# One layer of convolution blocks and experts on one core: the first norm in halves, fifteen weight loads moved beside the first scans, and the order of the expert tiles' pieces, patterns and result transfers changed

## The chip, the cores and the metric

The kernel runs on 1 core of one Trainium2 chip. The metric is the device time in microseconds (us) of one execution; for the kernel before it is the median of 3 runs. Engines are named as the profile names them: PE (TensorE), DVE (VectorE), ACT (ScalarE), POOL (GpSimd), and SP (SyncE), which here only issues DMAs.

## The reference

Four images of 256 channels and 32x32 pixels (1024 positions) go through one convolution block and one mixture of experts. Everything is float32. Cut to what matters:

```python
# conv block, per image; xs: 1024 positions x 256 channels, already normalised over C
xn = layernorm(xs)                                  # again, with norm_w, norm_b
xc = 4 branches of 64 channels
# one branch (mamba), 128 inner channels, 16 states:
u, z = split(xc @ inw.T);  u = silu(causal_conv4(u))
dt, Bm, Cm = u @ xpw.T;    dt = softplus(dt @ dtw.T + dtb)
h[t] = exp(dt[t]*A) * h[t-1] + dt[t]*u[t]*Bm[t]     # the selective scan, t = 0..1023
y[t] = sum over states of h[t]*Cm[t]
xm = (y + u*D) * silu(z) @ outw.T + skip*xc
# then: sigmoid gate Q over the branches, three 1-d convolutions with products (r, f),
# local convolution || 8-head attention over 1024 positions, product fc, layernorm, gelu,
# norm over the image, 3x3 depthwise convolution, layernorm, product proj
x = x + conv_block(ln_c(x))
# experts: t = 4096 tokens x 256
t = t + MoE(ln_t(t))   # 8 experts, top 2 by softmax, 256 -> 1024 -> gelu -> 256
```

## The kernel before

**Stages.** `network()` places all weights, then everything is emitted under one `tc.manual_schedule`, so that on each engine the instructions run in the order in which the Python code calls them. The order is made by hand: the scans are the main line, and generators carry the other work beside them. `beat()` advances every running generator by ticks: each `yield n` asks to be left alone for n ticks, `pace(b, f)` changes how many ticks a generator of image b gets for one beat, and a generator's first beat advances it twice.

**Weights.** `load` puts each weight on a queue named in the call (SP, ACT or POOL) ahead of everything else; `wqkT_s`, `qk_b`, `vb`, `fcT_s` and others are among them. Six short preparations follow (`ob`, `prb`, `projT_s`, `fcm`, `fcT_s`, `fcb`: small products on PE, sums and scalings on DVE). `weights()` (L251) then builds `inwk`, the in-projection with the four taps of the causal convolution folded in (per branch a scaling `diag` on DVE, matmuls on PE, a copy on DVE), and `wd` from transposes of `xpw`.

**The opening.** `normalised(b)` (L382) fetches the image x in one DMA on SP, forms mean, centred values, squares, variance and root for each half of 512 positions (the squares on POOL), scales over the whole width with POOL and DVE, and stores `xl` in `XL`, a copy in DRAM for later. `first_part()` (L602) does for image 0, branch 0: both halves of `up` (`project_u`, 16 matmuls, L439), both silus, one load of the logarithm's function table on ACT (`log_exp`), `project_dt` (L470), `softplus`, `sum_dt` and `times_u` on POOL, and `spread_dt` (L499): DMAs on SP which broadcast dt over the states, through DRAM.

**The scans.** A part is one image, one branch, one half of 512 positions; 4x4x2 = 32 parts of 16 steps. A step holds the decay exp(dt*A) on ACT (L531), two groups of `dBu` (L538) and scan (L545) on DVE, the product with Cm (L550) on POOL with a copy of the last column (L549), and the sum over states as matmuls (L556). `scan(at, i, stop)` (L631) mixes in the next part's projections by three tables (`before`, `behind`, `group`).

**Beside the scans.** While image b is scanned, the generators of image b-1 (convolutions, attention, `joined`, `around`, `sent_off`) run. After the last scan, image 3's own chain stands alone: attention, product (`joined`), norm, 3x3 taps, norm, routing. Beside it run the pieces of expert tiles whose rows are there.

**Experts.** `dispatch` (L1435) computes the two experts of each token of an image, then sends its rows into `XS`, sorted by expert, by 16 indirect DMAs on POOL (L1560), each behind a small `memset` of a tile `apart`. `blank_ends` (L1389) writes 8 sets of blank rows behind the last counts, on ACT's queue, for the last image. The tiles of 256 rows come in `SERIES` (8, 8, 23): series s can start when the counts of image s+1 are known. `tiles()` (L1088) walks through them; its `load` calls `series`, which makes the table of tiles (`tiles_of`, `table`, L1582 to L1620; patterns by iota on POOL at L1582 and L1603, comparisons on DVE). Tile 15 is held until image 3's rows are sent (L1144). Each tile is emitted in 8 pieces, so many ticks apart as `PACE` (L1211) says for the stage in which image 3's chain is:

```python
PACE = {"product": 3, "norm": 1.7, "taps": 0.67, "rows": 1.6}
```

`tile()` (L1769) does 32 matmuls `h` (L1778), gelu on ACT (L1783), 32 matmuls `y` (L1788), the weighting `ys` (L1798) and two indirect DMAs on POOL which add 128 rows each to `Y` in DRAM (L1799); the second waits for the first, since both write `Y`. The last four tiles run only if the counts need them. `bring_back` (L1805) reads `Y` back (L1810) and adds it to the tokens.

Of the kernel before, what the change touches and what calls it, by code (L numbers as in the profile page):

```python
# [9 lines left out]
F32 = mybir.dt.float32  # L10
# [13 lines left out]
NHC = DFF // P  # L24

# [46 lines left out]
def network(  # L72
# [34 lines left out]
    def ps_tile(name):  # L107

        return psum.tile([P, HALF], F32, tag="ps", name=name)
# [33 lines left out]
    with tc.tile_pool(name="w_conv", bufs=1) as wp, tc.tile_pool(  # L143
# [11 lines left out]
        def load(ap, name, eng):  # L155
            t = wp.tile(list(ap.shape), F32, name=name)
            eng.dma_start(t, ap)
            return t
# [3 lines left out]
        moutT_s = load(moutT, "moutT_s", nc.scalar)  # L162
        qdwT_s = load(qdwT, "qdwT_s", nc.gpsimd)
        qpwT_s = load(qpwT, "qpwT_s", nc.gpsimd)
        rpwT_s = load(rpwT, "rpwT_s", nc.gpsimd)
        fpwT_s = load(fpwT, "fpwT_s", nc.gpsimd)

        wqkT_s = wp.tile([P, NC2, 4, P], F32, name="wqkT_s")
        for ci in range(NC2):
            nc.sync.dma_start(  # L170
                wqkT_s[:, ci].rearrange("p w (i x) -> p (w i) x", x=2 * HD)
                .rearrange("p c (i x) -> p c i x", x=HD),
                wqkT[:, ci].rearrange("p c (i x) -> p c i x", x=2 * HD)[:, :, :, 0:HD],
            )
        qk_b = wp.tile([P, 4], F32, name="qk_b")
        for i in range(4):
            at = _AT["qk_b"] + i // 2
            nc.scalar.dma_start(
                qk_b[ts(i, HD), :], vecs[ds(64 * (i % 2), HD), at : at + 8 : 2]
            )  # L180
        wvT_s = load(wvT, "wvT_s", nc.gpsimd)
        aoutT_s = load(aoutT, "aoutT_s", nc.gpsimd)
        fcT_s = load(fcT, "fcT_s", nc.sync)
        projT_s = load(projT, "projT_s", nc.gpsimd)

        vb = wp.tile([P, NC2], F32, name="vb")
        nc.scalar.dma_start(vb, vbias.rearrange("a (c p) -> p (a c)", p=P))
        ob = wp.tile([P, NC2], F32, name="ob")
        obp = ps_tile("obp")
        for co in range(NC2):  # L190
            for ci in range(NC2):
                nc.tensor.matmul(
                    obp[:, co : co + 1], aoutT_s[:, ci, ts(co, P)], vb[:, ci : ci + 1],
                    start=(ci == 0), stop=(ci == NC2 - 1),
                )
        nc.vector.tensor_tensor(
            ob, obp[:, 0:NC2], V[:, _AT["attn_outb"] : _AT["attn_outb"] + NC2], ALU.add
        )

        prb = wp.tile([P, NC2], F32, name="prb")  # L200
        prp = ps_tile("prp")
        for co in range(NC2):
            for ci in range(NC2):
                nc.tensor.matmul(
                    prp[:, co : co + 1], projT_s[:, ci, ts(co, P)], col("norm_b", ci),
                    start=(ci == 0), stop=(ci == NC2 - 1),
                )
        nc.vector.tensor_tensor(
            prb, prp[:, 0:NC2], V[:, _AT["proj_b"] : _AT["proj_b"] + NC2], ALU.add
        )  # L210
        for ci in range(NC2):
            nc.vector.tensor_scalar(
                projT_s[:, ci, :], projT_s[:, ci, :], col("norm_w", ci), None, ALU.mult
            )

        fcm = wp.tile([P, 2 * NC2, 1], F32, name="fcm")
        nc.vector.tensor_reduce(fcm, fcT_s, AX.X, ALU.add)
        nc.vector.tensor_scalar(fcm, fcm, 1.0 / C, None, ALU.mult)
        nc.vector.tensor_tensor(
            fcT_s, fcT_s, fcm.to_broadcast([P, 2 * NC2, C]), ALU.subtract  # L220
        )
        fcb = wp.tile([P, NC2], F32, name="fcb")
        fbp = ps_tile("fbp")
        for c in range(NC2):
            nc.tensor.matmul(
                fbp[:, 0:1], ones_mean, col("fc_b", c), start=(c == 0), stop=(c == NC2 - 1)
            )
        nc.vector.tensor_tensor(
            fcb, V[:, _AT["fc_b"] : _AT["fc_b"] + NC2], fbp[:, 0:1].to_broadcast([P, NC2]),
            ALU.subtract,  # L230
        )
# [141 lines left out]
        LEFT = KC - 1  # L373

# [5 lines left out]
        XN, XM = {}, {}  # L380

        def normalised(b):  # L382


            xn = XN[b] = act8.tile([P, NC2, N + LEFT], F32, tag="a8", name=f"xn_{b}")
            nc.gpsimd.memset(xn[:, :, 0:LEFT], 0.0)
# [4 lines left out]
            nc.sync.dma_start(xn[:, :, LEFT:], x[b].rearrange("(c p) n -> p c n", p=P))  # L391
# [92 lines left out]
        def sum_dt(b, n, h):  # L484
            both = T[b, n, h, "dt"] = actd.tile([P, 2, HALF], F32, tag="dt", name=f"dt_{b}_{n}_{h}")
            nc.gpsimd.tensor_tensor(both[:, 0, :], T[b, n, h, "low"], T[b, n, h, "over"], ALU.add)

        def times_u(b, n, h):
            both = T[b, n, h, "dt"]
            nc.gpsimd.tensor_tensor(  # L490
                both[:, 1, :], both[:, 0, :], T[b, n, "u"][:, half(h)], ALU.mult
            )
# [109 lines left out]
        def first_part():  # L602

            for h in range(2):
                project_u(0, 0, h)
            u = T[0, 0, "u"] = a4("u_0_0")
            for h in range(2):
                nc.scalar.activation(
                    u[:, half(h)], T[0, 0, h, "up"], AF.Silu, bias=col("convb", 0)
                )  # L610
            loaded[0] = None
            log_exp()
            project_dt(0, 0, 0)
            softplus(0, 0, 0)
            sum_dt(0, 0, 0)
            times_u(0, 0, 0)
            for g in range(GD):
                spread_dt(0, 0, 0, g)
            for h in range(2):
                project_c(0, 0, h)  # L620
                copy_c(0, 0, h)
            spread_c(0, 0, 0, 0)
            spread_b(0, 0, 0, 0)
            for h in range(2):
                project_z(0, 0, h)
                copy_z(0, 0, h)
            T["z"] = [(0, 0, "z")]
            for i in range(LEAD):
                decay(0, 0, 0, i)
# [416 lines left out]
        def sent_off(b):  # L1046
# [32 lines left out]
            pace(b, PACE["rows"])  # L1079
            yield from experts.dispatch(  # L1080
                b, xr, act8.tile(experts.XR, F32, tag="a8", name=f"XR_{b}"), root,
                log_exp,
            )
# [4 lines left out]
        def tiles():  # L1088
# [5 lines left out]

            def known(n):
                return experts.counted >= B - 3 + order[n][0]
# [4 lines left out]
            def load(n):  # L1101
                s, i = order[n]
                if i == 0:
                    tables.append(experts.series(
                        s, lambda name, shape: act2.tile(shape, F32, tag="a2", name=name)
                    ))
# [32 lines left out]
            for n in range(len(order)):  # L1139
# [3 lines left out]

                while n == sum(experts.SERIES[:2]) - 1 and not sent(n + 1):  # L1144
                    ahead(n + 1, 0)
                    yield 1
# [64 lines left out]
        PACE = {"product": 3, "norm": 1.7, "taps": 0.67, "rows": 1.6}  # L1211
        with tc.manual_schedule(engines=ALL):
            log_exp()
            start(normalised(0), weights())
            drain()
            first_part()
            for b in range(B):
                for p in range(PARTS):
                    at = b * PARTS + p
                    stop = b > 0 and p == PARTS // 2 - 1 or at == len(parts) - 1  # L1220
                    if b == 0 and p == 2:
                        start(normalised(1))
# [65 lines left out]
class Experts:  # L1288
# [9 lines left out]

    T = 256
# [6 lines left out]
    def __init__(self, ctx, tc, psum, B, b1, ident, eps5, ones_mean, Wg, bg, W1, W2, b2, out):  # L1306
# [13 lines left out]
        self.Y = md.tile([NTOK + P, C], F32, name="Y")  # L1320
        m0 = self.m0 = ctx.enter_context(tc.tile_pool(name="moe0", bufs=1))

        blank = self.blank = m0.tile([P, self.ROW], F32, name="blank")
        nc.gpsimd.memset(blank, 0.0)
        nc.gpsimd.iota(
            blank[:, C : C + 1], [[0, 1]], base=NTOK, channel_multiplier=1,
            allow_small_or_imprecise_dtypes=True,
        )
        nc.gpsimd.memset(blank[:, C + 3 : C + 4], -1.0)
        nc.scalar.dma_start(self.Y[ds(NTOK, P), :], blank[:, 0:C])  # L1330
# [43 lines left out]
        self.counted = -1  # L1374
        self.read = []
        self.blank_rows(self.SPARE)

    def blank_rows(self, at):

        ins = self.nc.scalar.dma_start(  # L1380
            self.XS[ds(at, self.T), :].rearrange("(n p) c -> p n c", p=P),
            self.blank.rearrange("p (a c) -> p a c", a=1)
            .to_broadcast([P, self.T // P, self.ROW]),
# [51 lines left out]
    def dispatch(self, b, X1, XR, root, log_exp):  # L1435
# [120 lines left out]
        apart = m0.tile([P, 1], F32, tag="apart", name=f"apart_{b}")  # L1556
# [21 lines left out]
    def tiles_of(self, temp, name, rows, base=0):  # L1578

        nc, K = self.nc, self.NTOK // self.T  # L1580
        steps = temp(f"steps_{name}", [P, NE, K])
        nc.gpsimd.iota(  # L1582
            steps, [[0, NE], [self.T, K]], base=base, channel_multiplier=0,
            allow_small_or_imprecise_dtypes=True,
        )
# [5 lines left out]
    def table(self, temp, keep, name, n, ntile, done=None):  # L1591
# [10 lines left out]
        which, past = temp(f"which_{name}", S), temp(f"past_{name}", S)  # L1602
        nc.gpsimd.iota(  # L1603
            which, [[1, n], [0, NE]], base=0, channel_multiplier=0,
            allow_small_or_imprecise_dtypes=True,
        )
# [28 lines left out]
    def series(self, s, temp):  # L1635
# [10 lines left out]
        ntile = self.tiles_of(temp, s, self.count[:, :, b : b + 1], 0 if last else T - 1)  # L1646
        if s:
            nc.vector.tensor_tensor(ntile, ntile, self.done, ALU.subtract)
        table, starts, ends = self.table(temp, self.kept, s, n, ntile, self.done if s else None)
# [119 lines left out]
    def tile(self, j, got, hs, ys):  # L1769
# [27 lines left out]
        for t in range(2):  # L1797
            nc.vector.tensor_scalar(ys[:, t, :], ys[:, t, :], wgt[:, t, :], None, ALU.mult)  # L1798
            nc.gpsimd.indirect_dma_start(  # L1799
# [3 lines left out]
            )  # L1803

# [122 lines left out]
```

## Time and profile before

| | us |
|---|---|
| runs | 2487.04, 2480.68, 2478.96; median 2480.68 |
| profiled execution, own time | 2486.92 (span 2485.2, mean granted PE clock 0.913) |
| first `dBu` (L538) / first scan (L545) | 80.13 / 80.93 |
| last group of `dBu` (L538) | 1676.3 |
| image 3 behind its attention: product, norm, taps, norm, routing | 1964 to 1992, 2020, 2044, 2083, 2110 |
| counts of image 3 known | 2109.94 |
| one expert tile in the last stretch | 14.25 |
| last result transfer issued / read-back issued | 2450.47 / 2455.74 |

All times come from the one profiled execution; its own time is 6.2 us above the median of the runs. Over the whole span PE is busy 85%, DVE 65%, ACT 48% and POOL 45%, but the shares differ by stage: DVE carries the scans, PE the attention and the tiles. In a row of the timeline the columns are start, duration, engine, line, operation, output<-inputs, shapes, count, and in brackets the idle time of the engine just before, with what ended it. PEclk is the share of full speed that the throttle granted to PE.

### The profile page before, as it was taken

How to read it: one execution, taken by the hardware profiler on the slowest of the kernel's cores; microseconds unless marked ns; L12 is line 12 of the kernel's file. 1: busy time of each engine (PE TensorE's matmuls, PEld its weight loads, DVE VectorE, ACT ScalarE, POOL GpSimd, SP SyncE). 2: the span in 40 equal slices, each digit the busy share in tenths (PEclk: the TensorE clock that was granted, in tenths of full speed). 3: DMA queues.
4: the chain of work that ended last, by engine and by line, in shares of the span. 5: the costliest groups of instructions: out<-in, count | busy, mean ns of one | idle time of the engine just before them, and what ended most of it. 6: DMA issues, size and time to landing. Idle time of an engine off the chain costs nothing. (4 is left out here: it accounts for less than half of the span.)

```text
span 2485.2 us, 28288 instructions
## 1 busy us (share of the span) xinstructions
PE 2122.3 (85%) x8810; PEld 941.7 (38%) x8810; DVE 1622.3 (65%) x2243; ACT 1193.9 (48%) x2016; POOL 1111.8 (45%) x1163
## 2 busy tenths in 40 slices
PE   5776778899977799998589999758999999599995
PEld 2121112333311132232013223204773477588884
DVE  2688998876799887789978877985424354111211
ACT  1544455368663647765253686413427654122221
POOL 2577777541577661176775405562112011322221
PEclk8799997899998889997788999868999999899997
DMA  3443342220243321033333202334431154566664
GB/s 95 99 109 93 96 117 70 72 70 27 51 103 97 75 61 34 28 105 98 97 80 77 57 18 51 90 100 145 115 112 36 55 154 142 176 195 196 190 195 148
DMA packets 154541, 244.17 MB, mean 98 GB/s; under 512 B 34017, under 2 KB 103301, under 8 KB 154377
## 3 DMA queue, kind: packets, MB, share of 16 engines
q1 hardware_dynamic: 133856, 215.46, 30.7%
q0 software_dynamic: 13744, 19.31, 3.8%
q10 hardware_dynamic: 6776, 7.45, 0.9%
q8 instruction: 74, 1.21, 0.2%
q14 instruction: 91, 0.74, 0.1%
HBM read 141.16 MB, written 33.85 MB: 70 GB/s over the span
## 5 line engine op out<-in xcount | busy, mean ns | idle before, releaser
L550 POOL TENSOR_TENSOR hs<-hs,cs 128x512 f32<-128x512 f32 x512 | 669.5, 1309 | 222.0 <-DVE hs L545 175.1
L556 PE MATMUL yp<-hs,quads 128*32 128x512 f32 x1024 | 344.5, 684 | 173.1 <-POOL hs L550 123.2
L531 ACT ACTIVATE dA<-dts,A 128x512 f32<-128x512 f32 x512 | 342.9, 713 | 291.6 <-DMA dts<-dt 185.7
L538 DVE TENSOR_TENSOR dBu<-dts,bs 128x512 f32<-128x512 f32 x512 | 348.1, 680 | 80.5 <-DMA dts<-dt 24.2
L545 DVE TENSOR_TENSOR_SCAN hs<-dA,last,dBu 128x512 f32<-128x512 f32 x256 | 327.7, 1280 | 24.9 <-DVE dBu L538 0.5
L1799 POOL DMA_INDIRECT Y<-ys,dest x70 | 112.6, 1609 | 512.7 <-DVE ys L1798 362.2
L545 DVE TENSOR_TENSOR_SCAN hs<-dA,dBu 128x512 f32<-128x512 f32 x256 | 312.5, 1221 | 30.6 <-ACT dA L531 5.7
L1783 ACT ACTIVATE hs<-h,b 128x256 f32<-128x256 f32 x280 | 117.0, 471 | 405.5 <-PE h L1778 265.6
L871 ACT ACTIVATE e<-st 128x512 f32<-128x512 f32 x512 | 263.1, 606 | 87.2 <-PE st L861 86.7
L1788 PE MATMUL y<-w,hs 128*128 128x256 f32 x1120 | 259.6, 383 | 4.8 <-ACT hs L1783 4.8
L1778 PE MATMUL h<-xT,w 128*128 128x256 f32 x1120 | 253.2, 382 | 0.8 <-DVE xT L1756 0.8
L1788 PEld LDWEIGHTS y<-w,hs 128*128 128x128 f32 x1120 | 212.2, 192 | 43.4 <-issue 10.1
L1778 PEld LDWEIGHTS h<-xT,w 128*128 128x128 f32 x1120 | 213.3, 191 | 40.2 <-issue 9.7
L1756 DVE COPY xT<-xp 128x512 f32<-128x512 f32 x35 | 24.2, 692 | 297.8 <-PE xp L1755 297.8
L556 PEld LDWEIGHTS yp<-hs,quads 128*32 128x32 f32 x1024 | 55.6, 117 | 429.0 <-POOL hs L550 287.4
L523 PE MATMUL bs<-u,xpwT_s 128*32 128x512 f32 x1024 | 176.9, 670 | 40.6 <-DVE hs L545 23.6
L549 POOL COPY last<-hs 128x1 f32<-128x1 f32 x256 | 66.3, 259 | 318.0 <-DVE hs L545 309.5
L913 DVE TENSOR_TENSOR e<-e,e 128x512 f32<-128x512 f32 x256 | 171.4, 732 | 53.9 <-PE av L903 44.0
L861 PE MATMUL st<-qk 32*128 32x512 f32 x1024 | 194.0, 655 | 6.8 <-DVE hs L545 4.5
L439 PE MATMUL up<-xn,inwk 64*128 64x512 f32 x256 | 131.7, 659 | 15.6 <-DVE hs L545 9.2
L903 PE MATMUL av<-e,v 128*32 128x512 f32 x1024 | 142.7, 621 | 0.0
L861 PEld LDWEIGHTS st<-qk 32*128 32x128 f32 x1024 | 68.1, 188 | 132.4 <-issue 88.1
(271 smaller groups left out, 2499.3 us busy)
## 6 DMA issues: line engine op xcount, KB each, us to landing
w<-in_W_dram SPq DMA_DIRECT2D x136, 512.0 KB, 4.0
dts<-dt SPq DMA_DIRECT2D x512, 128.0 KB, 2.4
cs<-cd SPq DMA_DIRECT2D x512, 64.0 KB, 2.0
xs<-XS SPq DMA_DIRECT2D x35, 260.0 KB, 4.5
b<-in_b_dram SPq DMA_DIRECT2D x35, 128.0 KB, 4.2
xn<-in_x_dram SPq DMA_DIRECT2D x4, 1024.0 KB, 5.7
XL<-xl SPq DMA_DIRECT2D x8, 512.0 KB, 2.8
xl<-XL SPq DMA_DIRECT2D x4, 1024.0 KB
```

What stands on the lines that cost most here:

```text
L523: nc.tensor.matmul(bs[r], xpwT_s[:, n, s : s + 1].to_broadcast([P, 32]), T[b, n, "u"][:, half(h)], start=True, stop=True,)
L531: nc.scalar.activation(dA, T[b, n, h, "dts", g][:, 0, :], AF.Exp, scale=A[:, g, n, q : q + 1])
L538: nc.vector.tensor_tensor(dBu, T[b, n, h, "dts", g][:, 1, :], T[b, n, h, "bs", q], ALU.mult)
L545: nc.vector.tensor_tensor_scan(hs, T[b, n, h, "dA", i], dBu, 0.0 if h == 0 else last, ALU.mult, ALU.add)
L550: nc.gpsimd.tensor_tensor(hs, hs, T[b, n, h, "cs", q], ALU.mult)
L556: nc.tensor.matmul(T[b, n, h, "yp"][ts(g, 32)], quads, T[b, n, h, "hs", q * GD + g], start=(q == 0), stop=(q == GS - 1),)
L861: nc.tensor.matmul(sts[i], k[r, ts(kt, P)], q[r, half(h)], start=True, stop=not shifted)
L871: nc.scalar.activation(es[i], sts[i], AF.Exp, scale=1.0 / HD**0.5)
L903: nc.tensor.matmul(accs[0][ts(i, HD)], v8[:, kt, ts(4 * g + i, HD)], es[i], start=(kt == 0), stop=(kt == NK - 1),)
L913: nc.vector.tensor_tensor(first[i], first[i], es[i], ALU.add)
L1778: nc.tensor.matmul(hp[:, i, :], w1(c, k), xT[:, c, :], start=(c == 0), stop=(c == NC2 - 1))
L1788: nc.tensor.matmul(yp[:, ts(t, C)], hs[:, k, ts(t, P)], w2(k), start=(k == 0), stop=(k == NHC - 1))
```

## The change

Five parts of the code change; the work itself stays the same.

1. **Opening.** x of image 0 is the first DMA on SP, in two pieces of 128 channels. A new `first_normalised()` works on image 0 in halves throughout: the squares are taken by ACT, all scaling by DVE. `start(weights(), first_normalised())` replaces `start(normalised(0), weights())`. `first_part` does half 0 from `up` to the spreads of dt before half 1's `up`, with `sum_dt` and `times_u` on DVE; silu and the logarithm's table are loaded twice.
2. **Weights.** Calls of `load` without a queue go on a list; a generator `later_weights()`, started with the first scan part, issues them on SP, one for each tick, and then does the six preparations.
3. **Patterns.** `count_up` makes the two iotas of a series in advance: for series 0 when `tiles()` starts, for series 1 and 2 at the third tile of the series before.
4. **Result transfers.** The two indirect DMAs of a tile no longer wait for one another (each follows those of the tile before), with a memset of `apart` between them. Blank rows get distinct targets, so `blank` and `Y` grow by 128 rows.
5. **Pieces.** Other numbers in `PACE`, a stage "routing" of its own, and "rows" from the counts on; tile 15 is not held back any more.

```diff
+        place_xn(0)          # xn_0: memset of 3 columns on POOL, two DMAs on SP
+        later = []
...
+        def load(ap, name, eng=None):
             t = wp.tile(list(ap.shape), F32, name=name)
-            eng.dma_start(t, ap)
+            if eng is None:
+                later.append((t, ap))
+            else:
+                eng.dma_start(t, ap)
...
+        def later_weights():
+            nc.sync.dma_start(vb, vbias.rearrange("a (c p) -> p (a c)", p=P))
+            for t, ap in later:
+                nc.sync.dma_start(t, ap)
+                yield 1
...          # wqkT_s in 2 DMAs, qk_b in 4, then ob, prb, projT_s, fcm, fcT_s, fcb
+        def first_normalised():
+            xn = XN[0]
...
+            mean = [column_mean(f"mean_0_{h}", [part(c, h) for c in range(NC2)]) for h in range(2)]
+            var = []
+            for h in range(2):
+                sq = [a2(f"sq_0_{h}_{c}") for c in range(NC2)]
+                for c in range(NC2):
+                    nc.vector.tensor_tensor(part(c, h), part(c, h), mean[h], ALU.subtract)
+                    nc.scalar.activation(sq[c], part(c, h), AF.Square)
+                var.append(column_mean(f"var_0_{h}", sq))
+                yield 1
...
+            for h in range(2):
+                root(r1[:, half(h)], var[h], eps6)
+                root(r2[:, half(h)], var[h], eps11, scale=1.0 + 1e-5)
+                for c in range(NC2):
+                    nc.vector.tensor_tensor(xl[c][:, half(h)], part(c, h), r1[:, half(h)], ALU.mult)
+                    nc.vector.tensor_tensor(part(c, h), part(c, h), r2[:, half(h)], ALU.mult)
+                    nc.vector.tensor_scalar(
+                        part(c, h), part(c, h), col("norm_w", c), col("norm_b", c),
+                        ALU.mult, ALU.add,
+                    )
+                yield 1
...
         def first_part():
+            u = T[0, 0, "u"] = a4("u_0_0")
             for h in range(2):
                 project_u(0, 0, h)
-            u = T[0, 0, "u"] = a4("u_0_0")
-            for h in range(2):
                 nc.scalar.activation(
                     u[:, half(h)], T[0, 0, h, "up"], AF.Silu, bias=col("convb", 0)
                 )
-            loaded[0] = None
-            log_exp()
-            project_dt(0, 0, 0)
-            softplus(0, 0, 0)
-            sum_dt(0, 0, 0)
-            times_u(0, 0, 0)
-            for g in range(GD):
-                spread_dt(0, 0, 0, g)
+                loaded[0] = None
+                log_exp()
+                if h == 0:
+                    project_dt(0, 0, 0)
+                    softplus(0, 0, 0)
+                    sum_dt(0, 0, 0, nc.vector)
+                    times_u(0, 0, 0, nc.vector)
+                    for g in range(GD):
+                        spread_dt(0, 0, 0, g)
...
-            pace(b, PACE["rows"])
-            yield from experts.dispatch(
+            pace(b, PACE["routing"])
+            for ticks in experts.dispatch(
...
+                if experts.counted == b:
+                    pace(b, PACE["rows"])
+                yield ticks
...
+            experts.count_up(0, temp)
+            yield 5
...
-                while n == sum(experts.SERIES[:2]) - 1 and not sent(n + 1):
-                    ahead(n + 1, 0)
-                    yield 1
+                if order[n] in ((0, 2), (1, 2)):
+                    experts.count_up(order[n][0] + 1, temp)
...
-        PACE = {"product": 3, "norm": 1.7, "taps": 0.67, "rows": 1.6}
+        PACE = {"product": 4, "norm": 2.2, "taps": 0.9, "routing": 2, "rows": 0.75}
...
-            start(normalised(0), weights())
+            start(weights(), first_normalised())
...
+                    if b == 0 and p == 0:
+                        start(later_weights())
...
-        blank = self.blank = m0.tile([P, self.ROW], F32, name="blank")
+        blank = self.blank = m0.tile([P, T // P, self.ROW], F32, name="blank")
...
+    def count_up(self, s, temp):
...
+        self.numbers[s] = steps, which
...
-            nc.gpsimd.indirect_dma_start(
+        added = []
+        for t in range(2):
+            if t:
+                nc.gpsimd.memset(self.apart, 0.0)
+            ins = nc.gpsimd.indirect_dma_start(
                 out=self.Y[:, :],
...
+            for other in added:
+                self.tc.declare_no_dep(ins.ins, other.ins, reason="no two share a row")
+            self.follow(ins, self.added, "a row may be added to by both")
+            added.append(ins)
+        self.added = added
```

## The prediction

> **What bounds the kernel now.** I read the page first, then the busy time by stage, then the timeline of the first 130 us, of the last scan part and of everything behind the scans, and the waits of PE. The page's chain that ended last covers only the final 2 us, so the bound has to be read stage by stage.
>
> ```profile
> PE 2122.3 (85%) x8810; PEld 941.7 (38%) x8810; DVE 1622.3 (65%) x2243; ACT 1193.9 (48%) x2016; POOL 1111.8 (45%) x1163
> ```
> ```profile
> core 0: us, PE busy (x) PEld busy (x) DVE busy (x) ACT busy (x) POOL busy (x), PEclk, DMA share, GB/s
> 50.00:75.00 25.00, 20.76 (x31) 6.80 (x32) 2.45 (x2) 8.25 (x12) 7.98 (x6) 0.52 0.11 43
> 300.00:400.00 100.00, 76.86 (x231) 17.92 (x232) 93.92 (x101) 50.43 (x75) 77.46 (x88) 0.91 0.40 100
> 2300.00:2400.00 100.00, 100.00 (x479) 88.06 (x478) 17.96 (x59) 23.51 (x56) 21.59 (x14) 1.00 0.67 194
> ```
> No engine bounds the opening (DVE 2.45 of 25 us), DVE bounds the scans (94%), PE bounds the expert tiles at the end (100%).
>
> ```profile
> 34.41 2.82 PE L343 MATMUL mean<-xn,ones_mean 128*128 128x512 f32 x4
> 54.24 14.02 PE L439 MATMUL up<-xn,inwk 64*128 64x512 f32 x16 [6.35 <-POOL xn L421]
> 68.19 2.07 PE L470 MATMUL dtp<-u,wdt 128*128 128x512 f32 x2
> 75.56 10.14 SPq L499 DMA_DIRECT2D dts<-dt  x16
> 80.13 0.70 DVE L538 TENSOR_TENSOR dBu<-dts,bs 128x512 f32<-128x512 f32 x1 [22.71 <-DMA dts<-dt]
> ```
> The opening is one chain of latencies: mean, norm, both halves of up, dt, spread, first scan at 80.93. Nothing overlaps it.
>
> ```profile
> 1642.81 0.29 DVE L1586 TENSOR_TENSOR steps<-count,steps 128x128 f32<-128x128 f32 x1 [5.37 <-POOL steps L1582]
> 1649.13 1.27 POOL L550 TENSOR_TENSOR hs<-hs,cs 128x512 f32<-128x512 f32 x1 [6.18 <-DVE hs L545]
> ```
> In the last part the first tile table needs a pattern that sits behind scans and row transfers on POOL: DVE waits 5.37 us for it, then POOL 6.18 us for DVE.
>
> ```profile
> 2126.26 3.03 ACT L1783 ACTIVATE hs<-h,b 128x256 f32<-128x256 f32 x8 [15.52 <-DMA XS<-blank]
> 2126.78 3.72 PE L1788 MATMUL y<-w,hs 128*128 128x256 f32 x16 [2.83 <-ACT hs L1783]
> 2167.15 1.12 PE L1755 MATMUL xp<-ident,xs 128*128 128x128 f32 x4 [22.40 <-DMA xs<-XS]
> 2445.90 1.54 POOL L1799 DMA_INDIRECT Y<-ys,dest  x1 [7.79 <-DVE ys L1798]
> 2450.47 1.54 POOL L1799 DMA_INDIRECT Y<-ys,dest  x1 [3.03 <-DMA Y<-ys,dest]
> 2455.74 6.59 SPq L1810 DMA_DIRECT2D yy<-Y  x7
> ```
> Behind the attention of the last image PE stands 2.83 us for ACT, which queues behind eight blank-row transfers, and 22.4 us for the first rows of series 2. The last two result transfers follow one another 4.57 us apart, and the read-back follows the second.
>
> **Opening.** x now goes out first and later weights do not share the way; PE's first taps need only V and `every`. gm ends at 7.75 (row); in `beat` both generators advance twice on their first tick, so PE then runs two taps (2.06 each, DVE inwk 0.68 and diag 0.67 between): 13.3, by when x (1 MB, 8.6 us from issue under the old load) is in. Mean 2.82 and 1.88; centring of half 0 1.29, squares on ACT 2x0.57, var 1.9, four root steps 2.6: 22.8. DVE's six scaling passes (0.62 each, from 1.23 for 1024) and diag end at 27.4, the fourth taps at 28.4, four rounds of xpw and wd (37.08 to 42.6 with other work, 1.03 each) at 32.6. Eight up matmuls for half 0 at the 0.876 of the row, 7.0: 39.6. Silu 0.7 and the table load 1.28 (before it was paid after both halves), dtp 2.07, softplus 2.53 (70.31 to 72.84), two sums on DVE at 0.68 in place of 1.27 and 1.26 on POOL: the first dt spread leaves at 46.7 instead of 75.56. ACT now decides: up of half 1 ends at 49.5, its silu at 50.2, and a second pair of table loads (2x1.28) is added. From the second silu to the last z copy took 68.99 to 77.28, 8.3 us; 0 to 2.5 of it, the softplus, falls out, and the first decay (0.72) follows. The first scan starts at 57 to 60; I take 58.7, 22.2 us earlier. By then the spreads have landed: scans 0 to 4 took 9.5 us (80.93 to 90.44), paced by dts, and will take 4x1.92 = 7.7: 1.8 more. Together 24.0.
>
> The unknown is PE's clock in `up`. The row has it at half speed for 14 us of unbroken work (PEclk 0.50 from 52 to 72); at 106 us eight took 3.70. If half 0 and half 1 ran like that, 3.3 each and 1 of dtp go, about 8 us more. I take the slow row: the same xpw rounds, with PE nearly idle, stand ahead of it.
>
> The Trainium skill, page "TensorE: Matmul & The Clock Gate", Part 1, says that about 3.4 us of sustained matmuls return the clock to full. The row of `up` does not agree (16 matmuls of 64 rows, 14 us, never faster). By the rule half 0 would take an estimated 5.3 us and half 1 3.5, and the forecast would be some 6 us lower.
>
> **Weights beside the scan.** DVE gets fcm 1.22+0.16, fcT 1.22, ob, prb and fcb 0.16 each, projT 0.35+0.34: 3.8 us, in part 1, where it is busy 31.6 of 33.4 us: all of it on the path. PE's 4.6 us (obp, prp, fbp) hide, PE being at 77%. SP gets fifteen issues: wqkT 2.82, qk_b 4.35 and vb 0.45 (their old rows), fcT 0.4 to 2.98, seven others at 0.43 (weight issues of the tiles): 11 to 13.6 us, ahead of cs of quads 2 and 3 and of the dts of part 1. SP issues about 25 of part 0's 36 us, so it just fits; the last dts group lands about when step 3 of part 1 needs it. Cost 0 to 4, I take 1; if the cover were gone, all 13.6. The 2.4 MB find DMA at 59% share. XL[0] and the second x issue cost nothing: no one waits. Net opening: 24.0-3.8-1 = 19.2 (12 to 29).
>
> **Patterns.** The iotas of table 0 come five ticks before the table. DVE's 5.37 and POOL's 6.18 are one stall; the table's 4.2 us on DVE stay, but POOL (2.52 us a step against DVE's 1.98) hides most. Gain 5 (2 to 6). The two held act2 buffers leave 15; attention needs about 13. Free.
>
> **Result transfers.** The second of a tile's two no longer waits for the first. In the middle PE covers both already (14.25 us a tile). At the end 4.57 becomes 1.54 plus a memset (0.4 with its gap): 2.3 gained (1 to 3).
>
> **Tile pieces.** I counted the yields. Product, norm, taps, norm, routing have 12, 17, 10, 21, 19 ticks. At paces 3/1.7/0.67/1.7/1.6 that places tile 13, piece 5 at the count; at 4/2.2/0.9/2.2/2 it is tile 12, piece 1: 12 pieces, 22 us of PE (1.81 each), move behind the count, and 0.75 then puts tile 15 at the last row transfer without its wait. PE work is the same; only its idle time counts. Before: 7.6 in the stages, 2.83, 22.4 = 33. After:
> - Stages: the chain gets 13 us shorter, not 22: the taps alone are 20 us of DVE (16x1.25) and 4 of the tiles', over 11 pieces (20 us of PE). Idle 13 (9 to 20).
> - Blank rows: ACT's block (11.3 from the counts' end) now falls on pieces 1 or 2, where PE has only one or two h pieces left and y needs ACT: 9 (3 to 12).
> - First rows of series 2: load is still called from tile 15, its DVE work behind that tile's predecessor: ys 1.5, table 4.9, SP 5.3 (2155.3 to 2160.6), landing 6.5, against 10.8 of PE: 7.4 (3 to 9).
>
> Sum 29.4: 3 gained (-9 to +17).
>
> **Sum.** 19.2+5+2.3+3 = 29.5. The profiled execution took 2486.92 (span 2485.2), 6.2 above the median of the three runs, so its successor would be 2457.4; against the median 2480.68, **2451**.
>
> **Rivals.** *Tail as meant*: blank block covered as now and stage idle still 7.6; 15 of 33 idle remains, 18 gained in place of 3: 2436. For it: ACT's 15.5 us cost PE only 2.83 before. Against: the counted piece. *Fast halves*: up at 3.3 us less each: 2443. *Queue full*: all of SP's 13.6 on the scan, the tail at -9: 24-17.4+5+2.3-9 = 5 gained, 2476. *Starved PE* (slower): behind the attention the moved pieces leave pure idle, 22; the blank block goes uncovered, 12.7 more; the 22.4 stays; clock drops add 5: 40 lost against 26.5 gained elsewhere, 2494. It decides from 26.5 us of added idle between 1964 and 2170; against it, the stages held waits on PE (var, ACT behind gelu) that shrink. *Not as said*: x still arriving late behind POOL's memset would leave the opening near 70 us, about 2470.
>
> **Numbers.** Mine 0.56, tail as meant 0.20, fast halves 0.10, queue full 0.06, starved 0.06, not as said 0.02. About 0.3% (7.4 us) can be told from no change. Faster 0.88, same 0.06, slower 0.06. Range 2427 (6, 2.6 and some 15 more from tail or clock) to 2471 (opening 12 and the tail at its low end); queue full and starved lie outside.
>
> **What would show it.** First scan near 59; up in two runs of 8 at 0.88 with dtp between; no 5.37 in the last part; DVE 4 us longer in part 1; xs wait below 10, a wait of y on ACT near 9; result pairs 2 us apart. Wrong if the first scan starts after 70, or the idle time of PE behind the attention leaves 24 to 42.

## The result, and the profile after

The changed kernel takes 2480.34 us (median of 4), the kernel before 2480.61: ratio 0.9995, interval 0.9977 to 1.0013. No change can be seen, where 2451 was forecast. The profiled execution of after has a span of 2478.3 us.

The page's engine line and the stages, in the columns of before:

```profile
PE 2131.6 (86%) x8810; PEld 947.8 (38%) x8810; DVE 1631.0 (66%) x2255; ACT 1196.3 (48%) x2020; POOL 1101.3 (44%) x1182
```

The same 8810 matmuls now keep PE busy 9.3 us longer. The opening, from the timeline of after:

```profile
35.80 7.19 PE L496 MATMUL up<-xn,inwk 64*128 64x512 f32 x8
45.77 7.19 PE L496 MATMUL up<-xn,inwk 64*128 64x512 f32 x8
49.89 10.15 SPq L556 DMA_DIRECT2D dts<-dt  x16
59.86 1.22 DVE L602 TENSOR_TENSOR_SCAN hs<-dA,dBu 128x512 f32<-128x512 f32 x1 [2.40 <-ACT dA L588]
```

The first scan starts at 59.86, 21.1 us earlier, with `up` in two runs of eight around dt. So the opening did what it should. The first table, in the last scan part:

```profile
1623.57 0.94 DVE L1664 TENSOR_TENSOR steps<-count,steps 128x128 f32<-128x128 f32 x1
1624.86 3.26 DVE L1674 TENSOR_TENSOR_SCAN ends<-every,ntile 128x8 f32<-128x8 f32 x1
...
1629.02 1.70 DVE L1687 TENSOR_SCALAR expert<-expert 128x8 f32<-128x8 f32 x1
```
```profile
1626.81 1.27 POOL L607 TENSOR_TENSOR hs<-hs,cs 128x512 f32<-128x512 f32 x1
...
1629.38 1.27 POOL L607 TENSOR_TENSOR hs<-hs,cs 128x512 f32<-128x512 f32 x1
```

In the kernel before, `ends` and `expert` were:

```profile
1643.53 0.17 DVE L1596 TENSOR_TENSOR_SCAN ends<-every,ntile 128x8 f32<-128x8 f32 x1
1644.70 0.17 DVE L1613 TENSOR_SCALAR expert<-expert 128x8 f32<-128x8 f32 x1
```

The stall of 5.37 us is gone, but operations that took 0.29 (`steps`) and 0.17 (`ends`, `expert`) in the kernel before now take 0.94, 3.26 and 1.70; the last two end, to 0.1 us, when a product on POOL ends (1628.08 and 1630.65).

The waits of PE behind image 3's attention:

```profile
PE y L1865 <- ACT hs L1860: 12.3, 4, 7.7
PE xp L1832 <- DMA xs<-XS: 6.7, 1, 6.7
PE mean L371 <- DVE xi L1097: 4.7, 1, 4.7
PE var_fin L371 <- ACT sq_fin L1006: 4.1, 1, 4.1
PE places L1567 <- DVE oh L1560: 3.3, 1, 3.3
```

The columns are total, times and longest. The wait for the first rows of series 2 has fallen from 22.4 to 6.7, as forecast; the others have grown. The end:

```profile
2442.19 1.54 POOL L1881 DMA_INDIRECT Y<-ys,dest  x1 [10.42 <-DVE ys L1875]
2444.04 1.55 POOL L1881 DMA_INDIRECT Y<-ys,dest  x1 [0.19 <-POOLq L1769]
2449.06 7.97 SPq L1897 DMA_DIRECT2D yy<-Y  x8
```

The result pair is 1.85 us apart in place of 4.57.

**Where the time went.** The profiled execution of before lay 6.3 us above the median of its runs; a second one (before_again below, span 2479.8) is nearer to it. Against that one, after is 17.1 us ahead when the last scan ends (1655.8 against 1672.9), loses 18.7 from there to the last matmul of the tiles (785.1 against 766.4), gains 2.7 up to the read-back and 0.4 behind it: 1.5 in all. Of the 18.7, 15.2 are PE's busy time for the same work (739.6 against 724.5) and 3.5 idle time (45.5 against 41.9). The same stretch in all kernels, with times in us ("behind the scans" runs from the end of the last scan to the last tile matmul, PE's busy and idle time are those in it):

| kernel | last scan ends | behind the scans | PE busy | PE idle | wait for first rows of series 2 | ratio to before (interval) |
|---|---|---|---|---|---|---|
| before_again | 1672.9 | 766.4 | 724.5 | 41.9 | 22.4 | 0.9998 (0.9976 to 1.0019) |
| after | 1655.8 | 785.1 | 739.6 | 45.5 | 6.7 | 0.9995 (0.9977 to 1.0013) |
| old_pieces | 1654.2 | 750.3 | 722.1 | 28.2 | 7.3 | 0.9860 (0.9833 to 0.9887) |
| new_pieces_only | 1680.6 | 791.0 | 740.2 | 50.8 | 14.7 | 1.0102 (1.0069 to 1.0134) |
| filled | 1656.8 | 771.0 | 751.8 | 19.2 | 1.6 | 0.9952 (0.9938 to 0.9966) |
| old_stages | 1658.1 | 756.3 | 723.2 | 33.1 | 11.8 | 0.9880 (0.9858 to 0.9902) |
| old_patterns | 1650.7 | 756.1 | 723.9 | 32.2 | 12.1 | 0.9878 (0.9856 to 0.9899) |
| old_results | 1657.9 | 750.8 | 721.6 | 29.2 | 8.2 | 0.9877 (0.9851 to 0.9902) |
| opening_only | 1656.9 | 764.2 | 723.3 | 40.9 | 21.2 | 0.9933 (0.9916 to 0.9950) |

Each row is one profiled execution. With the same opening, the end of the last scan lies anywhere from 1650.7 to 1658.1, so a difference in that column is known to a few us only.

### The profile page after: what moved, and what is told of

It is laid out like the page before. It is cut to its first block, busy times and chain, and to the rows that moved or that the text cites. A ratio compares the mean times of both kernels' runs of the same rounds, so it can differ in the third digit from the quotient of the medians.

```text
span 2478.3 us, 28314 instructions
## 1 busy us (share of the span) xinstructions
PE 2131.6 (86%) x8810; PEld 947.8 (38%) x8810; DVE 1631.0 (66%) x2255; ACT 1196.3 (48%) x2020; POOL 1101.3 (44%) x1182
## 5 line engine op out<-in xcount | busy, mean ns | idle before, releaser
L1865 PE MATMUL y<-w,hs 128*128 128x256 f32 x1120 | 270.2, 394 | 12.3 <-ACT hs L1860 12.3
L1865 PEld LDWEIGHTS y<-w,hs 128*128 128x128 f32 x1120 | 219.7, 199 | 55.0 <-ACT hs L1860 14.4
L496 PE MATMUL up<-xn,inwk 64*128 64x512 f32 x256 | 138.8, 688 | 11.5 <-DVE hs L602 11.4
```

What stands on the lines that cost most here:

```text
L1865: nc.tensor.matmul(yp[:, ts(t, C)], hs[:, k, ts(t, P)], w2(k), start=(k == 0), stop=(k == NHC - 1))
```

## The experiments

**before_again**: no edit.

> The kernel before, unchanged, for a second profile. The profiled execution of before took 6.3 us more than the median of its runs. Theory 'clock' (behind the scans TensorE's granted clock falls to half after each idle gap, and this makes the time): ratio 1.000, and a profile near 2480 whose 6 us less lie in stretches at half clock, within the scans or behind the attention. Rival 'waits': the 6 us lie in one wait that was longer in the first profile (the 22.4 us for the first rows of series 2 foremost).

Ten executions took 2477.27 to 2493.17 us. The second profile has the same waits behind the scans (22.4 and 2.9); its last scan ends at 1672.9 in place of 1678.4, so the difference of the two spans, 5.4 us, lies wholly ahead of that. "Waits" falls; the difference is in the scans, one of the two places that "clock" named. Three of the 32 parts make most of it: the 11th (50.3 us against 47.7, granted clock 0.86 against 0.93), the 19th (50.3 against 47.8, 0.86 against 0.89) and the 25th (52.2 against 49.1, but 0.87 against 0.76). The longer part has the lower clock in two of the three only, so the clock is not shown as the cause.

**old_pieces**: part 5 alone undone.

```diff
+                while n == sum(experts.SERIES[:2]) - 1 and not sent(n + 1):
+                    ahead(n + 1, 0)
+                    yield 1
...
-        PACE = {"product": 4, "norm": 2.2, "taps": 0.9, "routing": 2, "rows": 0.75}
+        PACE = {"product": 3, "norm": 1.7, "taps": 0.67, "routing": 1.6, "rows": 1.6}
```

> The changed kernel with part 5 alone undone: PACE 3 / 1.7 / 0.67 / 1.6 again (1.6 in routing and behind the counts) and tile 15 held until the rows are sent. Theory 'pieces': the 15.6 us that the stretch from the last scan to the end grew by come from the new paces alone (15.3 us of it TensorE at half clock), so the time falls by 15 to 19 us, to 2461 to 2465, with no half-clock stretch between 1730 and the wait for the first rows of series 2. Rival 'transfers' (blank rows with distinct targets, result pairs side by side or the patterns cost it): stays within 4 us of 2480.

It took 2445.6 us: 34.7 less than before, twice what theory "pieces" expected. Behind the scans 34.8 us are saved against after, half of it idle time (28.2 against 45.5) and half the speed of the matmuls (722.1 against 739.6). The clock was full from the attention to the wait for the rows:

```profile
1941.10:2120.00 178.90, 168.26 (x726) 129.99 (x725) 76.52 (x207) 74.84 (x129) 48.14 (x59) 1.00 0.55 162
```

The surprise is the wait for the first rows of series 2: 7.3 us with the old paces. So parts 3 and 4 shorten it without the new paces. The new paces alone shorten it as well, to 14.7 in the next run, but beside parts 3 and 4 they add only 0.6 (6.7 in after).

**new_pieces_only**: the kernel before with the other side of that diff.

> The kernel before with part 5 alone: new PACE, routing stage, no hold of tile 15. Theory 'pieces': slower by 15 to 19 us, about 2497, with eight or so stretches at half clock behind the attention. Rival 'transfers': within 4 us of 2480. Rival 'only beside the other parts' (the paces cost time only because the opening moved the tiles): within 5 us as well, but then old_pieces gains.

2508.97 us, 28.7 slower. Busy time grows by 15.7 us and idle time by 8.9, in a kernel whose opening, patterns and transfers are old: the paces cost this by themselves. (The profiled execution is the slowest of the four; 7.7 us of it lie ahead of the end of the last scan, where the paces of image 3 do not act yet.) "Transfers" and "only beside the other parts" fall.

**filled**: the changed kernel, with idle matmuls in the waits, such as

```diff
+        FILL = {'var_lgn_3_0': 3, 'mean_3_0': 5, 'var_fin_3_1': 4}
...
         def column_mean(name, chunks):

             out = ps(name)
+            fill(out, FILL.get(name, 0))
```

> The changed kernel with idle matmuls (128x512, results overwritten) put on TensorE where it waits behind the attention: 3 ahead of the first var_lgn, 5 ahead of the first mean, 4 ahead of the second var_fin, 3 ahead of places, 8 behind the blank rows, 7 ahead of the first rows of series 2; 30 in all, 26 us of TensorE at full clock in gaps that sum to 29 us. Theory 'clock': the gaps keep their length but the clock stays at 1.0 behind the attention, so the matmuls between them run at full speed and 8 to 14 us are gained. Rival 'latency' (the chain of image 3 on VectorE and ScalarE sets the stage, matmul speed is hidden): 0, or slower by a few us where a filled gap runs over.

2468.74 us: 30 more matmuls make the kernel 11.6 us faster than before, and after was at 2480.34. The stretch behind the scans, columns PE, PEld, DVE, ACT, POOL, PEclk, DMA share and GB/s, in after and in filled:

```profile
1655.80:2440.90 785.10, 739.64 (x3398) 538.08 (x3398) 255.83 (x611) 281.92 (x541) 157.55 (x180) 0.96 0.46 136
```
```profile
1656.80:2427.80 771.00, 751.77 (x3458) 540.35 (x3458) 255.95 (x610) 281.89 (x541) 156.84 (x180) 0.98 0.48 138
```

The 30 calls are 60 matmul records of 0.43 us at full clock, 25.8 us. Without them PE is busy 726.0 us, as in the kernel before, and idle 45.0, as in after. So the gaps stayed and the work between them ran at nearly full speed (granted clock 0.98): 13.6 us of the 18.7 are the clock alone. "Latency" falls for this part.

**opening_only**: old_pieces with the patterns made as in the next run and the result transfers by the lines of the kernel before (no memset between them, the second waits for the first). The blank rows keep their distinct targets, here and in old_results.

> Parts 1 and 2 alone (norm and first part in halves, weights beside the scan); patterns, order of the result pairs and pieces as in the kernel before. Theory: the 22 us by which the last scan ends earlier all reach the end, 2457 to 2461. Rival 'given back': behind the scans something that does not depend on the opening sets the time, less than 15 us gained, above 2465.

2464.5 us, 16.7 less than before, between what the theory and its rival asked for; the last scan ends 16.0 us earlier than in before_again, and all of that reaches the end. "22 us" was read from the first profile of before. The wait for the rows stays at 21.2, and the trace shows its cause:

```profile
2128.21 0.86 POOL L1648 IOTA steps<- 128x128 f32 x1
```
```profile
2129.11 0.29 DVE L1662 TENSOR_TENSOR steps<-count,steps 128x128 f32<-128x128 f32 x1 [14.28 <-POOL steps L1648]
```
```profile
2144.73 1.12 PE L1831 MATMUL xp<-ident,xs 128*128 128x128 f32 x4 [21.16 <-DMA xs<-XS]
```

DVE waits 14.28 us for the pattern of series 2, which POOL reaches only behind the 16 row transfers and two result pairs, each pair with its wait of 3 to 7 us.

**old_patterns**: old_pieces with part 3 undone.

```diff
-            experts.count_up(0, temp)
-            yield 5
...
-                if order[n] in ((0, 2), (1, 2)):
-                    experts.count_up(order[n][0] + 1, temp)
...
+        self.count_up(s, temp)
         steps, which = self.numbers.pop(s)
```

> old_pieces (the changed kernel with the old paces and the hold, 2445.6 us) with part 3 undone too: the two iotas again stand on POOL just ahead of each table. In old_pieces the wait for the first rows of series 2 is 7.3 us instead of 22.4, though the paces are the old ones. Theory 'patterns far ahead': that is because the table of series 2 no longer waits for POOL to issue 16 row transfers and two results (iota at 2149.63 in the kernel before), so the wait returns to 15 to 23 us and the time rises by 8 to 15, to 2454 to 2461; the first table costs nothing either way (last scan part 42 us as in all runs). Rival 'results': the wait stays near 7, since the result pairs no longer hold POOL; within 3 us of 2445.6.

2449.55 us; the wait rises to 12.1. Against old_pieces the ratio intervals overlap, so the time decides nothing. The wait lies between what the two theories asked for.

**old_results**: old_pieces with the second result transfer behind the first.

```diff
-            for other in added:
-                self.tc.declare_no_dep(ins.ins, other.ins, reason="no two share a row")
-            self.follow(ins, self.added, "a row may be added to by both")
+            self.follow(ins, added or self.added, "a row may be added to by both")
```

> old_pieces with part 4 undone: the second result transfer of a tile waits for the first again. Theory: at the end 3 us are lost (4.6 between the last two transfers in place of 1.9), and behind the counts the row transfers stand behind two such waits on POOL (up to 7 us each), so the first rows of series 2 come later by up to 7: 2449 to 2456. Rival 'results alone made the short wait for the rows': 2458 or more, with old_patterns unchanged.

2452.08 us, as expected of the theory, though here too the ratio interval overlaps that of old_pieces, with 10.8 us from the last matmul to the read-back in place of 8.3; the wait for the rows is 8.2. Reading the three together: without parts 3 and 4 the wait is 21.2, with results alone 12.1, with patterns alone 8.2, with both 7.3. Each of these is one profile. Either part takes POOL's queue out of the way of the table; they do not add up.

**old_stages**: after with the four stage paces of before only.

```diff
-PACE = {"product": 4, "norm": 2.2, "taps": 0.9, "routing": 2, "rows": 0.75}
+PACE = {"product": 3, "norm": 1.7, "taps": 0.67, "routing": 1.6, "rows": 0.75}
```

> The changed kernel with the four old stage paces (3, 1.7, 0.67, routing 1.6), but 'rows' 0.75 from the counts on and no hold of tile 15. Theory 'stages': the wider spacing before the counts alone costs the 35 us between 2480 and 2445.6, so this is within 4 us of old_pieces. Rival 'behind the counts': the faster pace and the missing hold push the row transfers back behind results of tiles, 2452 to 2465.

2453.68 us: 26.7 of the 34.7 us come back, busy time is whole again (723.2) and idle time 33.1. The spacing ahead of the counts is the main cost. The time is 8 us above old_pieces, where "stages" allowed 4, and in the range of its rival. What is left lies behind the counts, in the wait for the rows (11.8 against 7.3); in the time itself the intervals of old_stages and old_pieces overlap.

**port**: old_pieces with a stretch behind everything, on small tiles `sm` (64 columns), large tiles `big` (512) and a PSUM tile `bank` (`bench` in the rows); its total time is not compared.

```diff
+        def small(n):
+            for _ in range(n):
+                nc.vector.tensor_scalar(sm[2], sm[0], 2.0, None, ALU.mult)
+                nc.vector.tensor_tensor(sm[2], sm[0], sm[1], ALU.mult)
+                nc.vector.tensor_reduce(
+                    sm[2][:, 0:8], sm[0].rearrange("p (a b) -> p a b", b=8), AX.X, ALU.add
+                )
+                nc.vector.tensor_tensor_scan(
+                    sm[2], sm[0], sm[1], 0.0, ALU.mult, ALU.add
+                )
+                nc.vector.tensor_tensor(sm[2], bank[:, 0:64], sm[1], ALU.mult)
...
+        small(3)
...
+        for _ in range(16):
+            nc.gpsimd.tensor_tensor(big[2], big[0], big[1], ALU.mult)
+        small(3)
```

> old_pieces with a stretch of its own behind everything: VectorE does 3 rounds of five small operations on 64 columns (scalar multiply, product of two SBUF tiles, sum, scan, product of a PSUM and an SBUF tile) alone, and 3 rounds beside 16 products of 512 columns on GpSimd (1.3 us each). In the changed kernel the first table's operations, of about 0.2 us, took 0.94 (steps), 3.26 (ends, a scan) and 1.70 (expert, a scalar operation), each ending when a product on GpSimd ended. Theory 'held back': beside GpSimd the scalar operation, the product and the scan take up to 1.3 us or a multiple, the sum and the product with PSUM stay at about 0.2. Rival 'one unlucky wait': all five take the same time alone and beside it.

One round alone, and one beside POOL:

```profile
2449.15 0.20 DVE L1355 TENSOR_SCALAR sm<-sm 128x64 f32<-128x64 f32 x1
2449.38 0.23 DVE L1356 TENSOR_TENSOR sm<-sm,sm 128x64 f32<-128x64 f32 x1
2449.64 0.22 DVE L1357 TENSOR_REDUCE sm<-sm 128x8 f32<-128x64 f32 x1
2449.89 0.29 DVE L1360 TENSOR_TENSOR_SCAN sm<-sm,sm 128x64 f32<-128x64 f32 x1
2450.29 0.23 DVE L1363 TENSOR_TENSOR sm<-bench,sm 128x64 f32<-128x64 f32 x1
...
2455.58 0.95 DVE L1355 TENSOR_SCALAR sm<-sm 128x64 f32<-128x64 f32 x1
2456.56 1.34 DVE L1356 TENSOR_TENSOR sm<-sm,sm 128x64 f32<-128x64 f32 x1
2457.93 0.22 DVE L1357 TENSOR_REDUCE sm<-sm 128x8 f32<-128x64 f32 x1
2458.18 1.12 DVE L1360 TENSOR_TENSOR_SCAN sm<-sm,sm 128x64 f32<-128x64 f32 x1
2459.34 0.22 DVE L1363 TENSOR_TENSOR sm<-bench,sm 128x64 f32<-128x64 f32 x1
```

Scalar operation, product and scan go from 0.20 to 0.29 us to 0.95 to 1.34; the sum and the product with PSUM stay at 0.22. "Held back" stands. The Trainium skill, page "SBUF — State Buffer", section "Who interferes with whom", has the same division: a VectorE operation with two SBUF inputs contends with a GpSimd instruction that reads SBUF, a scalar operation can do so, and a reduction, or an operation with one SBUF input outside the two-port modes, does not. The run agrees with it in all five kinds.

**weights_opening** and **old_pieces_again**: the fifteen issues and the sum, mean and subtraction of `fcT_s` moved into the opening (`fetch_weights` and `centre_fc`).

```diff
+            fetch_weights()
             first_part()
...
                 if h == 0:
+                    centre_fc()
                     project_dt(0, 0, 0)
```

> old_pieces with the fifteen later weights issued on SP ahead of the first up, and the sum, mean and subtraction on fcT (2.6 us of VectorE) beside the first softplus, where VectorE waits. Theory 'cover': the second scan part shrinks from 35.5 to 33 us, the first scan stays within 1 us of 60; 2 to 3 us gained against old_pieces. Rival 'SP': the issues (11 to 14 us) push the spreads of dt back, the first scan at 62 to 66, nothing gained or up to 4 lost.

> The changed kernel with part 5 undone once more, beside weights_opening, for a narrower interval. Both theories: 0.984 to 0.988 of the kernel before.

2451.22 us (0.9867, 0.9851 to 0.9884) against 2448.52 (0.9866, 0.9850 to 0.9883): no difference. In the trace the second part is 33.0 us long in place of 35.5 and the first scan starts at 60.2, as "cover" expected; the first part is 1.4 us longer (33.1 against 31.7 in old_pieces_again). The gain is too small for this measurement. The version that beats both kernels is old_pieces, 0.9860 and 0.9866 in two sets of runs.

## Why the prediction was wrong

The forecast added up to 29.5 us gained; between the profiles of before_again and after it is 1.5. Nearly all that is missing lies behind the scans, where 3 gained were forecast and 18.7 lost were found, 15.2 of them in the term that the prediction put at nothing with the words "PE work is the same; only its idle time counts".

**Opening: right, 2 us large.** Forecast 58.7 and a net gain of 19.2; the first scan starts at 59.86 (the four rounds of xpw and wd took 5.8 us, not 4.1), and the last scan ends 17.1 us earlier than in before_again, which the scatter of that end covers. "SP just fits" held: DVE waits for no DMA in part 1. DVE's 3.8 us cost 2.5 in part 1 (35.5 against 33.0). The third part was 43.7 us in after and 39.1 in old_pieces, with the same code at granted clocks of 0.77 and 0.91; that is part of the scatter.

**Patterns: the place was wrong.** The step "POOL hides most" put 5 us of gain into the last scan part; it is 42.0 us long in place of 42.2. I took the stall as time lost on both engines. It was also the time in which the table had POOL out of its way: 5.37 us of wait went, and the table took 9.1 us (1623.57 to 1632.64) in place of 4.15. The gain of this part lay at the table of series 2, which I didn't price under it.

**Result transfers: right at the end, wrong in the middle.** 2.3 forecast, 2.7 found. "In the middle PE covers both already" looked at PE's queue; the waits were on POOL's queue, ahead of row transfers and the pattern.

**Tile pieces: forecast 3 gained, found 34.8 lost** (after against old_pieces). Four steps failed.
- *The base.* I counted the fall of the rows' wait from 22.4 to 7.4 as a gain of the pieces. The size was right (6.7), the cause wrong: with parts 3 and 4 the old paces have 7.3, and without them the new paces have 14.7. That alone turns +3 into 12 lost.
- *"The chain gets 13 us shorter."* From the end of the attention to the counts it took 145.9 us in before_again, 154.7 in after and 146.0 in old_pieces: with 86 tile matmuls fewer beside it in after than in before_again (about eleven pieces of 8), it got longer. Some 6 of the 8.7 us arise in the routing, where the chain's operations stand in order behind the tiles' on DVE, and the tiles' operations wait for matmuls at half clock:

```profile
2083.88 0.69 DVE L1833 COPY xT<-xp 128x512 f32<-128x512 f32 x1 [4.68 <-PE xp L1832]
...
2094.11 0.69 DVE L1870 TENSOR_TENSOR ys<-y,b 128x512 f32<-128x512 f32 x1 [3.45 <-PE y L1865]
...
2096.38 0.17 DVE L1605 COPY count<-acc 128x8 f32<-128x8 f32 x1
```

- *Stage idle 13 (9 to 20).* The gaps sum to 20.5: 2.60, 2.87, 1.45, 4.65, 4.10, 1.49 and 3.34. The blank rows took 7.7 (forecast 9).
- *The clock.* "PE work is the same; only its idle time counts" is the step that failed most. PE's gaps from the attention to the first rows of series 2 sum to 34.9 us in after and 33.0 in before_again, inside the 24 to 42 that was named as a sign; but PE's busy time for the same matmuls grew by 15.2 us against before_again and 17.5 against old_pieces (739.6 against 724.5 and 722.1), and 13.6 of it came back in filled. My own case put this at nothing, the rival "starved PE" at 5. Windows of after, with the first gap and two of the stretches behind gaps (columns as above):

```profile
1969.42:1972.02 2.60, 0.00 (x0) 0.00 (x1) 0.00 (x0) 2.56 (x6) 0.00 (x0) 1.00 0.74 257
1973.30:1976.70 3.40, 3.40 (x8) 2.21 (x7) 0.00 (x0) 2.54 (x5) 0.00 (x0) 0.50 0.00 0
2021.10:2027.90 6.80, 4.68 (x9) 3.11 (x10) 3.28 (x8) 1.26 (x2) 0.00 (x0) 0.50 0.00 0
```

A gap of 2.60 us, then PE fully busy at half clock. Before, the one long wait of 22.4 us cost the clock once, and mostly while PE had nothing to do: from 2149.3 to 2173.0 the clock was 0.50 with PE busy 5.85 of 23.7 us, and from 2173 it was 1.00. One half-clock stretch of after follows no gap: PE was busy throughout the 4.10 us ahead of it, mostly on matmuls with 8 columns (`gate`):

```profile
2072.87:2076.97 4.10, 4.10 (x34) 4.10 (x32) 0.52 (x3) 2.63 (x5) 0.00 (x0) 0.84 0.95 268
2075.70:2082.50 6.80, 6.80 (x21) 5.72 (x21) 1.73 (x8) 0.06 (x1) 0.00 (x0) 0.50 0.58 190
```

The rival "starved PE", with 40 us lost at a chance of 0.06, came nearest to the 34.8 found, but in part by luck: it put 35 of the 40 on idle time and 5 on the clock, where 17.3 and 17.5 were found (after against old_pieces), it kept the wait of 22.4, and by its own sign, 26.5 us of added idle time, it fails. That after comes out level with before, and not 13 us slower as in that rival, is due to the 15 us which parts 3 and 4 saved at the rows' wait, and which no case of mine counted apart from the pieces.

**What stays open.** Why the third scan part is 39 us long in some executions and 44 in others, with the clock at about 0.9 or 0.77, was not tried; nor why the clock falls behind the `gate` matmuls in after, while old_pieces has 1.00 over the whole stretch around the same matmuls; nor which of the stage gaps of part 5 costs most.

## What to carry to other kernels

Filler work beside a latency chain should be dense: spread thinner, it left the chain no shorter here, and the gaps took TensorE's clock down for the work that remained. When a wait has several queues ahead of it, find who issues the thing waited for and what stands before it there (POOL's pattern, not the late rows); then remove one cause at a time, because two fixes of one wait do not add up and a third change can be credited with their gain. A stall in which two engines wait for one another may also be what keeps them from disturbing each other.

## What the runs showed of the hardware

TensorE's granted clock was 0.50 after idle gaps of 2.6 to 4.7 us, in stretches of 3.4 and 6.8 us above, and the 30 overwritten matmul calls of filled in the gaps gave back 13.6 us of PE's busy time. It also stayed at 0.50 in the opening, from 38 to 55 us, with PE busy 16.22 of 17 us, most of it on the 64-row matmuls of `up`:

```profile
38.00:55.00 17.00, 16.22 (x22) 4.78 (x24) 1.38 (x2) 8.42 (x11) 0.00 (x0) 0.50 0.21 47
```

The Trainium skill, page "TensorE: Matmul & The Clock Gate", Part 1, puts the fall behind about one idle window of 3.4 us and the rise behind about 3.4 us of sustained work. Both differ here, and the measurements decide: the row of the first gap shows the fall after 2.60 us of idleness, and the line above shows no rise in 17 us.
